# Turned tiles kept interleaved: wide runs through DRAM, and products that read every fourth or eighth element

## The chip, the cores and the metric

The kernel runs on one core of a Trainium2 chip. The metric is the device time of one execution in microseconds, taken as the median of three runs. The times below that are called profiled come from one further execution, recorded by the hardware profiler.

The core has a matrix engine (TensorE, PE in the profile), whose weight loads are shown apart (PEld), a vector engine (VectorE, DVE), a scalar engine (ScalarE, ACT), a general one (GpSimd, POOL) and a queue that issues the transfers (SyncE, SP). A matmul has a stationary operand, which a weight load brings into the array, and a moving operand, which streams through it.

## The reference

64 graphs share one 256x256 adjacency matrix `adj`; each has 256 nodes with 128 features, all in float32. Four layers follow one another, each as `x = layernorm(x + layer(x))`:

```python
# layer 0, five steps (a gated recurrent unit on the graph)
m_in = einsum('nm,bmd->bnd', adj, h)          # m_out is the same, both matrices are adj
u3 = h @ u3_w.T + u3_b
z = sigmoid(av @ w3_w.T + w3_b + u3)          # av = concat(m_in, m_out)
r = sigmoid(av @ w4_w.T + w4_b + u3)
hv = tanh(av @ w5_w.T + w5_b + (r * h @ u5_w.T + u5_b))
h = (1 - z) * h + z * hv
# layer 1: softmaxed mask A; diagonal with W[0], the rest with W[1], and a bias
# layer 2: attention over the edges, times adj, then a two-layer network with norms
# layer 3: sum over k = 0..3 of adj^k x V_k (two equal Chebyshev stacks)
```

## The kernel before

The 64 graphs are taken as 32 pairs. One pair's activations are a tile of 128 partitions and 512 floats: four pieces of 128x128 (two graphs, two halves of the nodes each). The tile exists in two layouts. In the token layout, partitions are nodes; in the feature layout, partitions are features. A matmul contracts over the partitions, so a product with a weight matrix wants the feature layout and a product with `adj` wants the token layout, and the kernel turns tiles from one to the other all the time.

**How a tile is turned (`turn`, L557).** For the last pairs TensorE does it against an identity (L566). For all others it goes by DMA, in four steps: VectorE transposes the tile in blocks of 32x32 (L572, `STREAM_TRANSPOSE`); SP sends the result to a DRAM tile `d` of class E (L574), written so that each of the four pieces lies in one block of 128x128; then four transfers (L580, one per group of 32 partitions) fetch it back with blocks and partitions exchanged. Each run of consecutive bytes fetched is 32 floats, 128 bytes. What comes back is the turned tile with its four pieces one after another along the partition. One tile per pair, the attention weights `u`, is twice as wide (1024 floats, eight pieces) and is turned in the same way, back into itself.

**Where turned tiles are read.** `h` in layer 0, steps 2 to 5 (by `spread7`, L596, or by `spread`, L585, for the first pair; after the fifth step only by the addition at L755); `dT` in layer 1 (`products`, L758); `xT` in layer 2 (L824), the attention weights `wT` (L864) and `zT` (`products`); `xT` in layer 3 (`polynomial7`, L947, or L906 for the last two pairs). In all of these products the piece of the turned tile is the stationary operand, so it goes through a weight load.

**`spread7`** multiplies by a 256x256 matrix held as 2x2 blocks with seven products instead of eight. Three sums are formed first on VectorE or GpSimd (L615 to L617). Of the seven products (L609), three take a piece of the tile itself as stationary operand: `H(0, 0)`, `H(0, 1)` and `H(1, 1)`; four take a sum.

**Order of the work.** The program is not written in the order in which it runs. Each operation is handed to a planner (`Schedule`, L115) with an assumed duration for each engine that could do it. `order` (L163) picks, again and again, the ready operation that could start first and, among equals, the one that is due first, and fixes from this one order for every engine's queue. The list `SEEDS` (L63) perturbs the due times in each window of 15 us. For a transfer, the assumed times are a triple of wait, moving time and time after. Each queue on the chip then runs in that fixed order and waits on semaphores.

Of the kernel before, what the change touches and what calls it, by code (L numbers as in the profile page):

```python
# [12 lines left out]
P = 128  # L13
# [12 lines left out]
L1 = -1  # L26
# [36 lines left out]
SEEDS = [0, 113, 389, 2033, 10562, 18537, 0, 26210, 32078, 38683, 45160, 51706, 59435, 64921, 73141, 0, 83634, 0,  # L63
         0, 101285, 106383, 115324, 122347, 124837, 135500, 136596, 144091, 154692, 155685, 163406, 167552, 0,
         184910, 185838, 194559, 198013, 204219, 214550, 217961, 222675, 234550, 236036, 241268, 247877, 256254,
         259921, 269567, 275378, 0, 285335, 290367, 299853, 303332, 311190, 314874, 321452, 333089, 337426,
         340720, 349168, 0, 0, 0, 0, 0, 0, 0, 0, 0, 0, 0, 0, 426668, 0, 438032, 447771, 0, 460174, 0, 468597,
         475031, 0, 0, 497766, 503314, 0, 0, 520395, 524746, 0, 0, 545845, 549434, 555392, 562168, 571415, 574768,
         578884, 0, 0]
# [7 lines left out]
class Value:  # L77
# [3 lines left out]
    def __init__(self, cls=None, ap=None, name="v"):  # L81
        self.cls, self.ap, self.name = cls, ap, name
        self.writers, self.readers, self.left = [], [], 0


        self.seeded = self.full = False
# [153 lines left out]
def kernel(ctx: ExitStack, tc: tile.TileContext, x, xT, adj, adjT, mats, cols, rows, out):  # L240
# [305 lines left out]
    def tokens(v):  # L546
        return v.at(4, D)

    def to_sbuf(t, name):
        v = Value("A", name=name)  # L550
        evacuate(lambda: v.at(512), lambda: t.at(512), [t], [v])
        return v
# [4 lines left out]
    def turn(i, name, site, n=512):  # L557


        o = Value("A", name=name) if n == 512 else i  # L560
        if not by_dma(site):
            ts = [Value("PS", name="ps") for _ in range(n // 512)]
            for k, t in enumerate(ts):
                def fn(k=k, t=t):
                    for c in range(4):
                        nc.tensor.transpose(tokens(t)[:, c, :], i.at(n // P, P)[:, 4 * k + c, :], ident.ap)  # L566
                pe(TURN, fn, [i, ident], [t])
            for k, t in enumerate(ts):
                evacuate(lambda k=k: o.at(n)[:, 512 * k:512 * k + 512], lambda t=t: t.at(512), [t], [o])
            return o  # L570
        st, d = Value("A" if n == 512 else "B", name="turn"), Value("E", name="turn")
        dve(n / 512 * 0.55 + 0.09, lambda: nc.vector.transpose(st.at(n), i.at(n)), [i], [st])  # L572
        blocks = lambda *ap: bass.AP(tensor=d.ap.tensor, offset=d.ap.offset, ap=ap)
        S.add([("SP", 0.52, lambda: nc.sync.dma_start(blocks([P, P], [P * P, n // P], [1, P]), st.at(n // P, P)))],  # L574
              [st], [d], (0.6, n / 512 * 0.86, 0.5))

        def move():
            for q in range(4):
                b = blocks([P, 32], [32 * P, n // 32], [1, 32])
                nc.sync.dma_start(o.at(n // 32, 32)[32 * q:32 * q + 32],  # L580
                                  bass.AP(tensor=b.tensor, offset=b.offset + 32 * q, ap=b.ap))
        S.add([("SP", 2.1 if n == 512 else 2.7, move)], [d], [o], (-0.8, n / 512 * 1.5, 0.9))
        return o

    def spread(i, right):  # L585

        t = bank()
        for b in range(2):
            def fn(b=b):
                for j in range(2):  # L590
                    nc.tensor.matmul(t.at(2, N)[:, b, :], tokens(i)[:, 2 * b + j, :], right.ap[:, j, :],  # L591
                                     start=(b == j == 0), stop=(j == 1), skip_group_check=True)
            pe(mm(256, 2), fn, [i, right, *[t] * b], [t])
        return t

    def spread7(h, right, terms):  # L596
# [6 lines left out]
        H = lambda b, j: lambda: blk(h, 2 * b + j)  # L603
# [11 lines left out]
        sum_(0.335, 0.69, lambda e: e.tensor_sub(sv.at(4, P)[:, 0:2], h.at(4, P)[:, 0::2], h.at(4, P)[:, 2:4]), [h], [p1])  # L615
# [104 lines left out]
    def layer0(x0, hT):  # L720
# [34 lines left out]
        dve2(TT, lambda: nc.vector.tensor_add(y.at(512), h.at(512), x0.at(512)), [h, x0], [y])  # L755
        layer_norm(y, x0)

    def products(lefts, rights, t=None):  # L758

        first, t = t is None, t or bank()  # L760
        for c in range(4):
            def fn(c=c):
                for k, (i, w) in enumerate(zip(lefts, rights)):
                    nc.tensor.matmul(tokens(t)[:, c, :], tokens(i)[:, c, :], w(), start=(first and k == c == 0),  # L764
                                     stop=(k == len(lefts) - 1), skip_group_check=True)
            pe(mm(128, len(lefts)), fn, [*lefts, W1, *[t] * bool(c or not first)], [t])
        return t

    def layer1b(x1):
        xT = turn(x1, "xT", "x1")  # L770
        xb, rr = Value("A", name="xb"), Value("A", name="rr")
        dve_or_pool(lambda e: e.tensor_add(tokens(xb), tokens(x1), row("l1_bias", 4)), [x1, rbc], [xb])
        ts = []
        for i in range(2):
            t = bank()

            def fn(i=i, t=t):
                for b in range(2):
                    nc.tensor.matmul(t.at(2, 2, D)[:, :, b, :], tokens(xT)[:, 2 * b + i, :], W1.ap[:, i_w:i_w + 2, :], start=(b == 0),
                                     stop=(b == 1), skip_group_check=True)  # L780
            pe(mm(256, 2), fn, [xT, W1], [t])
            evacuate(lambda i=i: rr.at(2, N)[:, i], lambda t=t: t.at(512)[:, N:], [t], [rr], (0.28, 0.34))
            part = lambda t=t: t.at(2, 2, D)[:, 0]
            dve(0.335, lambda i=i, part=part: nc.vector.scalar_tensor_tensor(
                part(), part(), dcol.ap[:, i:i + 1], xb.at(2, 2, D)[:, :, i, :], op0=ALU.mult, op1=ALU.add), [t, dcol, xb], [t])
            ts.append(t)
        for i, t in enumerate(ts):
            def fn(i=i, t=t):
                for j in range(2):
                    nc.tensor.matmul(t.at(512)[:, :N], offT.ap[:, j, i * P:(i + 1) * P], rr.at(2, N)[:, j],  # L790
                                     start=False, stop=(j == 1), skip_group_check=True)
            pe(mm(256, 2), fn, [offT, rr, t], [t])
        s, rs = scale_stats([(t, range(i, 4, 2)) for i, t in enumerate(ts)])
        for i, t in enumerate(ts):
            scale_tokens(t, x1, range(i, 4, 2), s, rs)

    def layer1(x1):
        if S.pair >= n_pairs - L1:
            return layer1b(x1)
# [15 lines left out]
    def layer2(x2):  # L815
# [3 lines left out]
        for b in range(2):  # L819
            t = Value("PS", name="ps")  # L820

            def fn(b=b, t=t):
                for i in range(2):
                    nc.tensor.matmul(t.at(2, D + 2)[:, i, :], tokens(xT)[:, 2 * b + i, :], wpx.ap, start=True, stop=True)  # L824
            pe(mm(130, 2), fn, [xT, wpx], [t])
            dve(0.35, lambda b=b, t=t: nc.vector.tensor_add(hs()[:, 2 * b:2 * b + 2, :], t.at(2, D + 2),
                                                            hbias.ap[:, None, :].to_broadcast([P, 2, D + 2])), [t, hbias], [h])
# [32 lines left out]
        for b in range(2):  # L860
            def fn(b=b, t=t):
                for it in range(2):
                    for jt in range(2):
                        nc.tensor.matmul(tokens(t)[:, 2 * b + it, :], wT.at(8, P)[:, 4 * b + 2 * it + jt, :],  # L864
# [26 lines left out]
    def layer3(x3, p):  # L891
# [7 lines left out]
        for i in range(2):  # L899
            t = bank()  # L900

            def fn(i=i, t=t):
                for b in range(2):
                    c = 2 * b + i
                    pr = t.at(2, 2, D)[:, :, b, :]
                    nc.tensor.matmul(pr, tokens(xT)[:, c, :], vx.ap, start=(b == 0), stop=False, skip_group_check=True)  # L906
# [40 lines left out]
    def polynomial7(xT, qT, p):  # L947
# [5 lines left out]
        x0, x1, q0, q1 = (lambda: half(xT, 0)), (lambda: half(xT, 1)), (lambda: half(qT, 0)), (lambda: half(qT, 1))  # L953
# [4 lines left out]
        sum_(0.335, 0.69, lambda e: e.tensor_sub(S3(), x0(), x1()), [xT], [s3])  # L958
        sum_(0.335, 0.69, lambda e: e.tensor_sub(S2(), q1(), S3()), [qT, s3], [s2])
        sum_(0.335, 0.69, lambda e: e.tensor_add(S1(), x1(), q1()), [xT, qT], [s1])  # L960
# [4 lines left out]
        def product(v, k, left, right, r, start=False):  # L965
            def fn():
                for i in range(2):
                    nc.tensor.matmul(tokens(v)[:, 2 * k + i, :], left()[:, i * P:(i + 1) * P], right(), start=start and i == 0,  # L968
                                     stop=True, skip_group_check=True)
            pe(mm(128, 2), fn, [*r, vx, vq, vt, *[v] * (not start)], [v])  # L970

        VX, VQ, VT = (lambda k, v=v: (lambda: v.ap[:, k, :]) for v in (vx, vq, vt))
        R = lambda b: rr.at(2, 2, D)[:, :, b, :]
        blocks = lambda v, k: v.at(2, 2, D)[:, k]
        product(y, 0, x0, VX(0), [xT, s2], start=True)
        product(y, 1, S2, VT(1), [s2])
        product(t, 0, S1, VT(0), [s1], start=True)
# [3 lines left out]
        product(y, 1, S3, VT(2), [s3])  # L981
        product(y, 0, q0, VQ(0), [qT])
        evacuate(lambda: half(sv, 0), lambda: half(y, 1), [y], [sv], (0.28, 0.335))
        product(y, 1, q1, VT(3), [qT])
        dve(0.335, lambda: nc.vector.tensor_add(R(1), blocks(t, 0), blocks(sv, 0)), [t, sv], [rr])
        product(t, 0, S4, VQ(1), [s4])
# [103 lines left out]
```

## Time and profile before

| | |
|---|---|
| median of three runs | 1476.21 us (1476.14 to 1479.29) |
| the profiled execution | 1476.42 us |
| its span, first to last instruction | 1474.2 us |
| granted TensorE clock | 0.999 |
| TensorE busy | 1462.0 us in 8274 passes |
| weight loads | 8274, 1068.6 us busy, beside the matmuls |
| VectorE, ScalarE, GpSimd busy | 1293.2, 1078.7, 1010.0 us |
| DMA, queue of SP | 946704 packets, 214.81 MB, 71.3% of 16 engines |

One execution is profiled and its span, plus 2.2 us around it, is its time. Each float32 product of the program appears as two passes, each a weight load and a matmul, so the 512 products of L764 are 1024 in the profile. A row of groups gives the source line, the engine, the operation, the written and the read tiles by name (without buffer numbers), the shapes, the count, and after the bar the busy time in us and the mean duration of one in ns. Passes overlap, so count times mean is more than the busy time; the spacing of starts is what one pass costs.

### The profile page before, as it was taken

How to read it: one execution, taken by the hardware profiler on the slowest of the kernel's cores; microseconds unless marked ns; L12 is line 12 of the kernel's file. 1: busy time of each engine (PE TensorE's matmuls, PEld its weight loads, DVE VectorE, ACT ScalarE, POOL GpSimd, SP SyncE). 2: the span in 40 equal slices, each digit the busy share in tenths (PEclk: the TensorE clock that was granted, in tenths of full speed). 3: DMA queues.
4: the chain of work that ended last, by engine and by line, in shares of the span. 5: the costliest groups of instructions: out<-in, count | busy, mean ns of one | idle time of the engine just before them, and what ended most of it. 6: DMA issues, size and time to landing. Idle time of an engine off the chain costs nothing.

```text
span 1474.2 us, 29700 instructions
## 1 busy us (share of the span) xinstructions
PE 1462.0 (99%) x8274; PEld 1068.6 (72%) x8274; DVE 1293.2 (88%) x3185; ACT 1078.7 (73%) x3315; POOL 1010.0 (69%) x1574
## 2 busy tenths in 40 slices
PE   9999999999999999999999999999999999999998
PEld 6565666667667777777668777667777677778997
DVE  7877878889999989999988988888999889899995
ACT  3444556667788788878766887666788777889896
POOL 4422445566677788877658787657778788779875
PEclk9999999999999999999999999999999999999999
DMA  7544565767788898778786677675897777766653
GB/s 227 115 103 87 119 130 117 155 133 157 152 166 168 180 187 161 164 152 165 160 157 140 143 171 159 124 152 124 170 177 158 156 146 149 160 138 135 127 106 93
DMA packets 946868, 216.70 MB, mean 147 GB/s; under 512 B 726032, under 2 KB 942224, under 8 KB 946704
## 3 DMA queue, kind: packets, MB, share of 16 engines
q1 hardware_dynamic: 946704, 214.81, 71.3%
q8 instruction: 66, 1.08, 0.3%
q14 instruction: 98, 0.80, 0.2%
HBM read 116.86 MB, written 97.85 MB: 146 GB/s over the span
## 4 chain that ended last, share of the span: by engine, by line
PE 93%; DVE 3%; POOL 2%; ACT 1%; DMA 1%; issue 1%; SPq 0%; POOLq 0%; ACTq 0%; DVEq 0%
PE ps L609 24%; PE ps L735 9%; PE ps L742 9%; PE ps L743 9%; PE ps L727 9%; PE ps L728 9%; PE ps L764 7%; PE ps L968 6%; PE ps L864 3%; PE ps L1011 3%; PE ps L591 2%; PE ps L824 2%; POOL s L696 1%; DVE b L839 0%; POOL s L651 0%
## 5 line engine op out<-in xcount | busy, mean ns | idle before, releaser
L609 PEld LDWEIGHTS ps<-aT,a 128*128 128x128 f32 x2208 | 297.3, 192 | 78.2 <-issue 69.1
L273 ACT COPY a<-ps 128x128 f32<-128x128 f32 (+2 forms) x618 | 259.5, 442 | 105.2 <-PE ps L609 49.2
L609 PE MATMUL ps<-aT,a 128*128 128x128 f32 x2208 | 324.3, 275 | 0.5 <-ACT x L708 0.5
L731 ACT ACTIVATE a<-ps,bzrh 128x512 f32<-128x512 f32 x160 | 110.5, 691 | 102.4 <-PE ps L728 92.8
L746 ACT ACTIVATE ps<-ps,bzrh 128x512 f32<-128x512 f32 x160 | 106.2, 664 | 98.0 <-PE ps L743 95.6
L628 POOL TENSOR_TENSOR a<-a 128x128 f32<-128x128 f32 x206 | 105.2, 516 | 90.8 <-DVE a L624 80.1
L742 PE MATMUL ps<-a,w 128*128 128x512 f32 x320 | 163.8, 594 | 0.0
L728 PE MATMUL ps<-a,w 128*128 128x512 f32 x320 | 163.4, 592 | 0.0
L743 PE MATMUL ps<-a,u5h 128*128 128x512 f32 x320 | 163.4, 592 | 0.0
L735 PE MATMUL ps<-a,w 128*128 128x512 f32 x320 | 162.8, 594 | 0.1
L630 DVE TENSOR_TENSOR a<-ps,a 128x256 f32<-128x256 f32 x239 | 99.1, 417 | 71.0 <-ACT a L273 42.1
L688 ACT ACTIVATE a<-ps 128x128 f32<-128x128 f32 x504 | 133.1, 289 | 29.7 <-PE ps L764 13.4
L572 DVE STREAM_TRANSPOSE a<-a 128x512 f32<-128x512 f32 x215 | 149.4, 699 | 3.7 <-POOL a L1028 0.5
L696 POOL TENSOR_TENSOR s<-s,neg_half 128x4 f32<-128x4 f32 x127 | 142.4, 1122 | 6.8
L764 PE MATMUL ps<-W,a 128*128 128x128 f32 x1024 | 142.1, 275 | 0.1
L624 POOL TENSOR_TENSOR a<-a 128x256 f32<-128x256 f32 x123 | 92.0, 750 | 72.9 <-ACT a L273 72.1
L764 PEld LDWEIGHTS ps<-W,a 128*128 128x128 f32 x1024 | 130.3, 192 | 14.5 <-issue 12.4
L737 ACT ACTIVATE a<-ps,bzrh 128x512 f32<-128x512 f32 x160 | 110.8, 692 | 37.4 <-PE ps L735 34.3
L727 PE MATMUL ps<-a,W 128*128 128x512 f32 x256 | 131.0, 593 | 0.9 <-ACT a L273 0.9
L615 POOL TENSOR_TENSOR a<-a 128x256 f32<-128x256 f32 x97 | 72.3, 746 | 64.8 <-DMA a<-e 44.2
L743 PEld LDWEIGHTS ps<-a,u5h 128*128 128x128 f32 x320 | 60.8, 190 | 76.5 <-issue 64.8
L728 PEld LDWEIGHTS ps<-a,w 128*128 128x128 f32 x320 | 60.8, 190 | 76.5 <-issue 65.3
(255 smaller groups left out, 3650.7 us busy)
## 6 DMA issues: line engine op xcount, KB each, us to landing
e<-a SPq DMA_DIRECT2D x277, 256.0 KB
a<-e SPq DMA_DIRECT2D x1108, 64.0 KB
e<-b SPq DMA_DIRECT2D x32, 512.0 KB
b<-e SPq DMA_DIRECT2D x128, 128.0 KB
x<-x_in SPq DMA_DIRECT2D x32, 256.0 KB
t<-xT_in SPq DMA_DIRECT2D x32, 256.0 KB
a<-d SPq DMA_DIRECT2D x32, 256.0 KB
y_out<-a SPq DMA_DIRECT2D x31, 256.0 KB
```

Source lines behind the costliest of these rows:

```text
L273: S.add([("ACT", us[0], lambda: nc.scalar.copy(o(), i())), ("DVE", us[1], lambda: nc.vector.tensor_copy(o(), i()))], r, w)
L572: dve(n / 512 * 0.55 + 0.09, lambda: nc.vector.transpose(st.at(n), i.at(n)), [i], [st])
L609: pe(mm(128), lambda: nc.tensor.matmul(blk(t, k), left(), rt(), start=start, stop=True, skip_group_check=True), [*r, right, terms, *[t] * ...
L688: nc.scalar.activation(tokens(junk)[:, c, :], v.at(len(tiles), D)[:, k, :], AF.Square, scale=D ** -0.5, accum_out=mv()[:, c, 1:2])
L696: pool(1.02, lambda: nc.gpsimd.tensor_tensor(rs(), rs(), neg_half.ap, op=ALU.pow), [s, neg_half], [s])
L727: nc.tensor.matmul(t.at(512), mat("u3"), hT.at(512), start=True, stop=False)
L728: nc.tensor.matmul(t.at(512), w4.ap, mT.at(512), start=False, stop=True)
L735: pe(mm(512), lambda t=t, mT=mT: nc.tensor.matmul(t.at(512), w3.ap, mT.at(512), start=False, stop=True, skip_group_check=True), [w3, mT, t ...
L737: act(0.59, lambda t=t, z=z: nc.scalar.activation(z.at(512), t.at(512), AF.Tanh, bias=bzrh.ap[:, 0:1], scale=0.5), [t, bzrh], [z])
L742: nc.tensor.matmul(t.at(512), w5.ap, mT.at(512), start=True, stop=False)
L743: nc.tensor.matmul(t.at(512), u5h.ap, r.at(512), start=False, stop=True)
L764: nc.tensor.matmul(tokens(t)[:, c, :], tokens(i)[:, c, :], w(), start=(first and k == c == 0), stop=(k == len(lefts) - 1), skip_group_chec ...
```

## The change

Turned tiles are no longer stored as pieces one after another. After the change, element `f` of piece `c` lies at position `4 f + c` of the partition (`8 f + c` in the wide tile).

- VectorE's block transpose now takes the 32x32 blocks in the same order but writes its result with a step of four (eight) elements.
- The transfer to DRAM writes each partition as one run of 512 (1024) floats; each of the four transfers back reads runs of `n / 4`, so 128 (256) floats.
- The planner's assumed moving times for these two become 0.76 and 0.8 per 512 columns, from 0.86 and 1.5.
- A value that was turned by DMA is marked `turned`. Two helpers, `chunk` and `chunks`, give one piece or several in either layout, and every reader of a turned tile uses them. Sums over pieces (`spread7`, `polynomial7`, L755) read the turned tile with the step and write contiguously.
- `SEEDS` is a new list, and the unused variant `layer1b` (with the constant `L1`) is gone.

```diff
-SEEDS = [0, 113, 389, 2033, 10562, ...
+SEEDS = [0, 101, 386, 1734, 0, ...
-        self.seeded = self.full = False
+        self.seeded = self.full = self.turned = False
+    def chunk(v, c, n=4):
+        return v.at(P, n)[:, :, c] if v.turned else v.at(n, P)[:, c, :]
+    def chunks(v, *c):
+        return v.at(P, 4)[:, :, slice(*c)].rearrange("p f c -> p c f") if v.turned else v.at(4, P)[:, slice(*c)]
 def turn(i, name, site, n=512):
...
-        dve(n / 512 * 0.55 + 0.09, lambda: nc.vector.transpose(st.at(n), i.at(n)), [i], [st])
-        blocks = lambda *ap: bass.AP(tensor=d.ap.tensor, offset=d.ap.offset, ap=ap)
-        S.add([("SP", 0.52, lambda: nc.sync.dma_start(blocks([P, P], [P * P, n // P], [1, P]), st.at(n // P, P)))],
-              [st], [d], (0.6, n / 512 * 0.86, 0.5))
+        k, w = n // P, n // 4
+        dve(n / 512 * 0.55 + 0.09, lambda: nc.vector.transpose(st.at(4, 32, k).rearrange("p q e c -> p c q e"), i.at(k, 4, 32)), [i], [st])
+        line = lambda start, *ap: bass.AP(tensor=d.ap.tensor, offset=d.ap.offset + start, ap=ap)
+        S.add([("SP", 0.52, lambda: nc.sync.dma_start(line(0, [n, P], [1, n]), st.at(n)))], [st], [d], (0.6, n / 512 * 0.76, 0.5))
         def move():
             for q in range(4):
-                b = blocks([P, 32], [32 * P, n // 32], [1, 32])
-                nc.sync.dma_start(o.at(n // 32, 32)[32 * q:32 * q + 32],
-                                  bass.AP(tensor=b.tensor, offset=b.offset + 32 * q, ap=b.ap))
-        S.add([("SP", 2.1 if n == 512 else 2.7, move)], [d], [o], (-0.8, n / 512 * 1.5, 0.9))
+                nc.sync.dma_start(o.at(4, w)[32 * q:32 * q + 32], line(q * w, [n, 32], [32 * n, 4], [1, w]))
+        S.add([("SP", 2.1 if n == 512 else 2.7, move)], [d], [o], (-0.8, n / 512 * 0.8, 0.9))
+        o.turned = True
...
-        H = lambda b, j: lambda: blk(h, 2 * b + j)                       # spread7
+        H = lambda b, j: lambda: chunk(h, 2 * b + j)
-        sum_(..., lambda e: e.tensor_sub(sv.at(4, P)[:, 0:2], h.at(4, P)[:, 0::2], h.at(4, P)[:, 2:4]), [h], [p1])
+        sum_(..., lambda e: e.tensor_sub(sv.at(4, P)[:, 0:2], chunks(h, 0, 4, 2), chunks(h, 2, 4)), [h], [p1])
-        dve2(TT, lambda: nc.vector.tensor_add(y.at(512), h.at(512), x0.at(512)), [h, x0], [y])
+        dve2(TT, lambda: nc.vector.tensor_add(tokens(y), chunks(h, 0, 4), tokens(x0)), [h, x0], [y])
-                    nc.tensor.matmul(tokens(t)[:, c, :], tokens(i)[:, c, :], w(), ...     # products; likewise L591, L824, L906
+                    nc.tensor.matmul(tokens(t)[:, c, :], chunk(i, c), w(), ...
-                        nc.tensor.matmul(..., wT.at(8, P)[:, 4 * b + 2 * it + jt, :],
+                        nc.tensor.matmul(..., chunk(wT, 4 * b + 2 * it + jt, 8),
-        product(y, 0, x0, VX(0), [xT, s2], start=True)                    # polynomial7
+        product(y, 0, lambda i: chunk(xT, i), VX(0), [xT, s2], start=True)
```

## The prediction

> **What bounds the kernel now.** I read the page's busy times first, then the groups of TensorE by shape, then its timeline at two places, then the idle time by stage.
>
> ```profile
> PE 1462.0 (99%) x8274; PEld 1068.6 (72%) x8274; DVE 1293.2 (88%) x3185; ACT 1078.7 (73%) x3315; POOL 1010.0 (69%) x1574
> ...
> L609 PEld LDWEIGHTS ps<-aT,a 128*128 128x128 f32 x2208 | 297.3, 192 | 78.2 <-issue 69.1
> ...
> L609 PE MATMUL ps<-aT,a 128*128 128x128 f32 x2208 | 324.3, 275 | 0.5 <-ACT x L708 0.5
> ```
>
> TensorE is busy for 1462 of 1474 us, and 0.5 us of idle time stand before the 2208 passes of its largest group. Matmul ends are modelled, so I checked with the starts: over 1466.7 us from first to last pass, starts are 112 ns apart after a 128-wide pass (6446 passes), 216 after a 256-wide, 430 after a 512-wide. Those spacings fill 1462.6 us; what exceeds them is 8.8 us. So nothing is to be had from shorter waits beyond some 9 us, and anything that lengthens a pass is paid in full.
>
> What sets the 112 ns? First the timeline of weight loads and matmuls (start, length, engine, line), in the thick of it:
>
> ```profile
> 699.82 0.75 PEld L609 LDWEIGHTS ps<-aT,a 128*128 128x128 f32 x6
> ...
> 699.93 0.83 PE L609 MATMUL ps<-aT,a 128*128 128x128 f32 x6
> ```
>
> Six loads of 192 ns take 0.75 us: (750 - 192) / 5 = 112 ns apart; the matmuls likewise, (830 - 275) / 5 = 111. Load k+1 runs while pass k streams. Now a place where TensorE had been idle:
>
> ```profile
> 494.08 1.12 PE L727 MATMUL ps<-a,W 128*128 128x512 f32 x2 [0.90 <-ACT a L273]
> 495.05 1.02 PE L728 MATMUL ps<-a,w 128*128 128x512 f32 x2
> ...
> 495.05 0.19 PEld L728 LDWEIGHTS ps<-a,w 128*128 128x128 f32 x1 [0.24 <-issue]
> ```
>
> The two passes of L727 begin 0.97 us before the next pair, not 0.86: the first load lay bare. In the records the first spacing is 534 ns where 430 is usual. A contiguous load of 128 columns thus costs **104 ns** when nothing covers it, and a 128-wide pass covers 112. The slack is 8 ns. The last row shows that under 512-wide passes a load sits idle 0.24 us: it is fetched one pass ahead and no further, so slack of wide passes isn't saved up.
>
> Where TensorE is idle (stretch: length, PE busy, PEld, DVE, ACT, POOL, clock, DMA share, GB/s):
>
> ```profile
> 600.00:800.00 200.00, 200.00 (x1149) 145.83 (x1149) 180.75 (x433) 150.45 (x461) 145.63 (x231) 1.00 0.77 157
> ...
> 1400.00:1474.20 74.20, 68.13 (x511) 64.41 (x509) 55.63 (x170) 59.56 (x243) 47.46 (x77) 0.98 0.48 101
> ```
>
> None in the middle; half of the 12 us in the last stage.
>
> [...] the trace has 13.4 ns per 128 B packet against 29.5 per 512 B. No trace of before has a load, or a VectorE write, with such a step.
>
> **The change part by part.**
>
> *Stepped weight loads.* The program has 1064 products whose stationary operand was turned by DMA: layer 0 360 (three of seven, 30 pairs, four steps) and 16 for the first pair, dT 128, xT 120, wT 256, zT 116, layer 3 60 and 8. Of these 24 are 256 wide: 216 ns cover a doubled load. The other 1040 (784 at step four, 256 at eight) are two passes each, 2080. In the built order 106 of the first passes follow a 256- or 512-wide pass and are covered, which leaves 1974. Price per load: [...] 208 ns, **104 more**: 1974 x 0.104 = **+205 us**, all on TensorE's path. [...]
>
> *Stepped transposes.* 277 of 512 columns (699 ns) and 32 of 1024 (1228). [...] *Stepped sums and additions:* about 68 halves at L615 on VectorE, 32 of 512 columns at L755, some 60 small ones, [...] At nothing under a TensorE of 1474 + 205, which hides it; without that cover it is rival two. GpSimd's L615 (84 on tiles `a`, 746 ns) and its small sums grow too[...].
>
> *Transfers.* As many issues on SP (309 out, 1236 back, near 0.45 us each), no queue passed, no wait added. About 698,000 packets of 128 B become 142,000 of 512 B and 16,000 of 1 KB; the way out goes from 512 B to 2 and 4 KB. With the packets' times (13.4, 29.5, 55, 129 ns and some 220 for 4 KB) that is about 4.0 ms less over 16 engines, the share 71% down to 54%. Tiles land earlier; worth at most the 9 us above, of which the transfers are a part (in a chain over 480 to 540 us, their share is 8.5%). I take -2 to nothing, since the transpose ahead is as much later.
>
> *New order.* The same 4171 products and 1715 transfers; VectorE gets 40 instructions fewer, GpSimd 18 and ScalarE 11 more. About -8 and +13 us beside 181 and 464 idle: nothing. `layer1b` was never called.
>
> Sum: span 1474.2 + 205 = 1679, plus 2.2 around it: **1681 us**. The profiled execution (1476.4) is 0.2 above the median of the runs.
>
> **Rivals.**
>
> *One: a step of 16 bytes is free* on TensorE's load and on VectorE's write [...]. It decides if the stepped load stays under 112 ns, 8 above now. For it: half a microsecond more on transposes could vanish in 181 us of idle VectorE, and the transfers are truly lighter. [...] Then only the waits move: half of the 5 us lost between 200 and 1400 us and some of the last 6: **1471**, own range 1466 to 1480. This is the one on the other side.
>
> *Two: TensorE is free, VectorE is not.* [...] in an order made for 0.70 us transposes: about **1540**. [...]
>
> *Three: only the step of eight costs* [...]: 510 passes x 0.104 = 53, **1529**.
>
> **How the numbers follow.** 0.50 for the forecast (own range 1600 to 1765), 0.33 for rival one, 0.10 and 0.07 for the others. Below 1467 lies a tenth of rival one, above 1765 a sixth of the forecast case: the range is 1467 to 1765. Rival one splits into 0.19 faster, 0.08 same, 0.06 slower, by 0.2% (3 us, about what a measurement of this kernel can tell from no change); the rest is slower, 0.73.
>
> **What would show it.** Right: L609's loads with mean well over 192 ns and those of wT (L864) and dT most, starts near 216 ns apart behind them; loads in L728 or L743 unchanged; PE still at 99%; [...] DMA near 54%. Wrong: loads at 192 ns throughout; then read the transposes: at 0.70 it is rival one, above 1 us with TensorE idle on VectorE it is two. What I could have wrong most is the size: [...]

## The result, and the profile after

| | before | after |
|---|---|---|
| median of four runs | 1477.59 us (1476.14 to 1479.29) | **1715.79 us** (1713.68 to 1716.82) |
| ratio | | 1.161 (1.159 to 1.163) |
| profiled execution, its span | 1476.42, 1474.2 us | 1715.96, 1713.9 us |

The changed kernel is 16% slower, 238 us. The prediction was 1681 us in a range of 1467 to 1765, with 0.73 for slower; its likeliest case has happened, and its size is short by 35 us.

The page of the kernel after, busy times and groups (a row: line, engine, operation, tiles, shapes, count, then busy us and mean ns, then idle time ahead of it). All lines from `turn` on stand some lines lower or higher than before: L609 is now L615, L572 is L580, L864 is L840, L743 is L749.

```profile
PE 1701.8 (99%) x8274; PEld 1322.4 (77%) x8274; DVE 1428.7 (83%) x3145; ACT 1094.5 (64%) x3330; POOL 1026.2 (60%) x1592
...
L615 PEld LDWEIGHTS ps<-aT,a 128*128 128x128 f32 x2208 | 384.8, 235 | 73.0 <-issue 48.8
L615 PE MATMUL ps<-aT,a 128*128 128x128 f32 x2208 | 399.5, 310 | 3.5 <-POOL a L621 2.4
...
L580 DVE STREAM_TRANSPOSE a<-a 128x512 f32<-128x512 f32 x215 | 238.9, 1119 | 2.0 <-ACT a L714 0.2
...
L840 PE MATMUL ps<-h,b 128*128 128x128 f32 x512 | 131.0, 401 | 0.0
...
L840 PEld LDWEIGHTS ps<-h,b 128*128 128x128 f32 x512 | 126.6, 333 | 0.9 <-DVE s L651 0.2
L749 PEld LDWEIGHTS ps<-a,u5h 128*128 128x128 f32 x320 | 60.6, 190 | 77.3 <-issue 64.6
```

The same groups of loads and transposes in the kernel before:

```profile
L864 PEld LDWEIGHTS ps<-h,b 128*128 128x128 f32 x512 | 61.8, 192 | 1.1 <-DVE a L572 0.5 <-issue 0.5
L743 PEld LDWEIGHTS ps<-a,u5h 128*128 128x128 f32 x320 | 60.8, 190 | 76.5 <-issue 64.8 <-DVE a L630 1.2 <-DVE ps L748 1.0
...
L572 DVE STREAM_TRANSPOSE a<-a 128x512 f32<-128x512 f32 x215 | 149.4, 699 | 3.7 <-POOL a L1028 0.5 <-ACT a L708 0.4 <-PE ps L609 0.3
```

TensorE has the same 8274 passes and the same 99%, but is busy for 1701.8 us: it doesn't wait more, its passes take longer. The loads of L840, all stepped by eight, take 333 ns where they took 192, while those of L749, which no edit touched, stay at 190. The 235 of L615 is a mean over loads of two kinds, adjacent ones of 192 ns and stepped ones of 308 to 332. The block transposes went from 699 to 1119 ns.

The same eight products of the attention weights, one after another: weight loads in the timeline of the kernel before,

```profile
749.67 0.97 PEld L864 LDWEIGHTS ps<-h,b 128*128 128x128 f32 x8
```

and loads and matmuls in that of the kernel after:

```profile
906.04 1.99 PEld L840 LDWEIGHTS ps<-h,b 128*128 128x128 f32 x8
...
906.15 2.07 PE L840 MATMUL ps<-h,b 128*128 128x128 f32 x8
```

Before, (970 - 192) / 7 = 111 ns from load to load; after, (1990 - 333) / 7 = 237. The matmuls follow at the loads' pace, (2070 - 401) / 7 = 238: the array waits for weights.

Over the whole trace, 1986 passes of 128 or 130 columns start 180 to 280 ns before the next one, 233.7 on average; before there were 20. Their surplus over 112 ns is 241.7 us (before: 2.0). That is 239.7 more, and the span grew by 239.7.

### The profile page after: what moved, and what is told of

Its sections match the earlier page's. It is cut to its first block, busy times and chain, and to the rows that moved or that the text cites. A ratio compares the mean times of both kernels' runs of the same rounds, so it can differ in the third digit from the quotient of the medians.

```text
span 1713.9 us, 29595 instructions
## 1 busy us (share of the span) xinstructions
PE 1701.8 (99%) x8274; PEld 1322.4 (77%) x8274; DVE 1428.7 (83%) x3145; ACT 1094.5 (64%) x3330; POOL 1026.2 (60%) x1592
## 3 DMA queue, kind: packets, MB, share of 16 engines
q1 hardware_dynamic: 271504, 214.81, 40.9%
## 4 chain that ended last, share of the span: by engine, by line
PE 95%; DVE 2%; POOL 1%; issue 1%; DMA 0%; ACT 0%; SPq 0%; POOLq 0%; DVEq 0%; ACTq 0%
PE ps L615 25%; PE ps L770 10%; PE ps L748 8%; PE ps L749 8%; PE ps L741 8%; PE ps L733 8%; PE ps L734 8%; PE ps L840 7%; PE ps L945 6%; PE ps L800 3%; PE ps L989 2%; PE ps L597 1%; DMA W<-mats_in 0%; POOL a L621 0%; DVE a L580 0%
## 5 line engine op out<-in xcount | busy, mean ns | idle before, releaser
L615 PEld LDWEIGHTS ps<-aT,a 128*128 128x128 f32 x2208 | 384.8, 235 | 73.0 <-issue 48.8
L615 PE MATMUL ps<-aT,a 128*128 128x128 f32 x2208 | 399.5, 310 | 3.5 <-POOL a L621 2.4
L272 ACT COPY a<-ps 128x512 f32<-128x512 f32 (+2 forms) x625 | 261.7, 437 | 218.8 <-PE ps L615 126.0
L580 DVE STREAM_TRANSPOSE a<-a 128x512 f32<-128x512 f32 x215 | 238.9, 1119 | 2.0 <-ACT a L714 0.2
L770 PEld LDWEIGHTS ps<-W,a 128*128 128x128 f32 x1024 | 190.2, 255 | 15.1 <-issue 13.2
L770 PE MATMUL ps<-W,a 128*128 128x128 f32 x1024 | 201.1, 332 | 0.0
L630 POOL TENSOR_TENSOR a<-a 128x256 f32<-128x256 f32 x146 | 111.2, 765 | 108.2 <-ACT a L272 107.5
L749 PE MATMUL ps<-a,u5h 128*128 128x512 f32 x320 | 163.6, 593 | 0.1
L743 ACT ACTIVATE a<-ps,bzrh 128x512 f32<-128x512 f32 x160 | 110.5, 691 | 52.5 <-PE ps L741 47.6
L702 POOL TENSOR_TENSOR s<-s,neg_half 128x4 f32<-128x4 f32 x127 | 136.5, 1075 | 6.7
L840 PE MATMUL ps<-h,b 128*128 128x128 f32 x512 | 131.0, 401 | 0.0
L840 PEld LDWEIGHTS ps<-h,b 128*128 128x128 f32 x512 | 126.6, 333 | 0.9 <-DVE s L651 0.2
L749 PEld LDWEIGHTS ps<-a,u5h 128*128 128x128 f32 x320 | 60.6, 190 | 77.3 <-issue 64.6
```

The source lines that it names most:

```text
L272: S.add([("ACT", us[0], lambda: nc.scalar.copy(o(), i())), ("DVE", us[1], lambda: nc.vector.tensor_copy(o(), i()))], r, w)
L615: pe(mm(128), lambda: nc.tensor.matmul(blk(t, k), left(), rt(), start=start, stop=True, skip_group_check=True), [*r, right, terms, *[t] * ...
L702: pool(1.02, lambda: nc.gpsimd.tensor_tensor(rs(), rs(), neg_half.ap, op=ALU.pow), [s, neg_half], [s])
L749: nc.tensor.matmul(t.at(512), u5h.ap, r.at(512), start=False, stop=True)
L770: nc.tensor.matmul(tokens(t)[:, c, :], chunk(i, c), w(), start=(first and k == c == 0), stop=(k == len(lefts) - 1), skip_group_check=True)
L840: nc.tensor.matmul(tokens(t)[:, 2 * b + it, :], chunk(wT, 4 * b + 2 * it + jt, 8), hs()[:, 2 * b + jt, :D], start=(b == it == jt == 0), st ...
```

## The experiments

Eight kernels were run. In their diffs only the core of an edit is shown. Where one run stands for a kernel, it is the profiled one. Ratios are to runs of the kernel before that were taken beside each experiment (medians of 1476.4 to 1476.9 us).

**1. Only the loads put back.** In the changed kernel, products read adjacent elements.

```diff
-        product(0, H(0, 0), B(0, 0), [h], start=True)
+        product(0, L(0, 0), B(0, 0), [h], start=True)   # L: load_of(h, 2 * b + j); likewise at every product
+    def load_of(v, c, n=4):
+        return v.at(n, P)[:, c, :]
```

> The changed kernel, but every product reads the turned tile's pieces as 128 adjacent elements, as before the change (the products get wrong numbers; transposes, sums, transfers and order stay as changed). Theory (the stepped weight loads make the time, 121 ns more for each pass that nothing covers): all loads at 192 ns, passes 112 ns apart, and nearly all of the 238 us is gone: 1475 to 1510 us. What is left above 1476 is the price of VectorE's stepped writes without their cover: VectorE is then busy some 1429 of some 1490 us. Rival (the slower transposes or the new order hold TensorE up, the long loads only lie beside it): 1600 us or more.

Measured: 1518.18 us, 1.0278 (1.0258 to 1.0297) of before. 198 of the 238 us are gone, and the rest is more than was expected, by 8 us. From its page and its groups of TensorE:

```profile
PE 1478.7 (98%) x8274; PEld 1071.7 (71%) x8274; DVE 1415.7 (93%) x3145; ACT 1082.0 (71%) x3330; POOL 1046.9 (69%) x1592
...
L620 PE MATMUL ps<-aT,a 128*128 128x128 f32 x2208 | 325.4, 276 | 7.3 <-POOL a L626 3.0 <-DVE a L626 2.3 <-DVE a L628 0.7
L753 PE MATMUL ps<-a,w 128*128 128x512 f32 x320 | 164.2, 595 | 5.7 <-DVE a L761 2.6 <-DVE a L641 2.3 <-DVE a L864 0.6
```

The matmuls are back at 276 ns. VectorE is at 93% and TensorE now waits for it and for GpSimd (L626 is the first sum, L761 the end of a recurrent step). This is the second rival of the prediction, laid bare. Over the whole run VectorE is busy for 1416 of 1515 us, but that is an average. In two stretches (columns as in the prediction; the kernel before first, then this one)

```profile
400.00:600.00 200.00, 197.86 (x1149) 145.33 (x1148) 186.01 (x470) 163.82 (x522) 158.69 (x238) 1.00 0.86 171
```

```profile
400.00:600.00 200.00, 191.77 (x1099) 139.31 (x1098) 197.60 (x435) 156.31 (x497) 158.96 (x235) 1.00 0.53 162
...
1200.00:1400.00 200.00, 193.34 (x1215) 151.31 (x1214) 196.08 (x474) 159.48 (x551) 158.17 (x227) 1.00 0.45 136
```

VectorE is busy for 98 to 99% of the time, and TensorE loses 6.7 to 8.2 us in each. There VectorE's own time is the bound, or close to it. The order of work, which was planned with transposes of 0.64 us, may cost some of the rest; the two were not separated.

**2. Only the step put into the kernel before.**

```diff
-        product(0, H(0, 0), B(0, 0), [h], start=True)
+        product(0, L(0, 0), B(0, 0), [h], start=True)   # L: load_of(h, 2 * b + j); likewise at every product that reads a turned tile
+    def load_of(v, c, n=4):
+        return v.at(P, n)[:, :, c] if v.turned else v.at(n, P)[:, c, :]
...
+        o.turned = True
```

> The kernel before, with one thing of the change: products read the turned tile with a step of four, or eight for the attention weights (the tile isn't interleaved, so the numbers are wrong). Theory: some 1985 passes at 234 ns instead of 112, the rest as before: 1476 + 1985 x 0.122 = 1718 us, and VectorE's transposes stay at 0.70 us. Rival (the step costs only together with the slower transposes or the new order): below 1600.

Measured: 1709.71 us, once. 1979 passes have the long spacing, 233.8 ns on average, and VectorE's busy time is what it was:

```profile
PE 1699.8 (100%) x8274; PEld 1322.7 (77%) x8274; DVE 1297.1 (76%) x3185; ACT 1089.0 (64%) x3315; POOL 998.3 (58%) x1574
```

The step in the weight loads makes some 233 us of the 238 by itself, with old transposes, old transfers and old order.

**3. Only the transposes put back.**

```diff
-        dve(..., lambda: nc.vector.transpose(st.at(4, 32, k).rearrange("p q e c -> p c q e"), i.at(k, 4, 32)), [i], [st])
+        dve(..., lambda: nc.vector.transpose(st.at(n), i.at(n)), [i], [st])
```

> The changed kernel, but VectorE's block transposes write adjacent elements (the pieces come back wrongly arranged, so the numbers are wrong); stepped loads and sums stay. Theory (VectorE's slower transposes cost nothing as long as the stepped loads cover them, though 40 us without that cover): 1706 to 1716 us, as the changed kernel. Rival (the two costs add): 1716 - 40 = 1676.

Measured: 1709.83 us, once, with transposes of 699 ns and VectorE busy for 1317.5 us. So under the stepped loads the slower transposes cost some 6 us; it is one run, and the four of the changed kernel spread over 3 us. The costs don't add: with the loads put back as well (experiment 4) the time is 1474, against 1518 with the loads alone, so that without cover VectorE's steps, sums and addition included, cost 44.

**4. Only the transfers and the order.** Adjacent elements throughout:

```diff
-        dve(..., lambda: nc.vector.transpose(st.at(4, 32, k).rearrange("p q e c -> p c q e"), i.at(k, 4, 32)), [i], [st])
+        dve(..., lambda: nc.vector.transpose(st.at(n), i.at(n)), [i], [st])
-        o.turned = True
```

> The changed kernel without any step: transposes write, and sums and products read, adjacent elements; what stays is the wide runs through DRAM, the planner's new transfer times and the new order (the pieces are wrongly arranged, so the numbers are wrong). Theory: lighter transfers are worth at most the 9 us that TensorE's starts lose before: 1468 to 1478 us, DMA share near 46%, transposes at 0.70 us. Rival (the transfers are worth nothing, or the new order is worse): 1478 to 1490.

Measured: 1474.30 us over 22 runs, 0.9981 (0.9974 to 0.9988). That is 2.6 us, within the ceiling of some 9 us of late starts. To see which of its two parts gained them, both were crossed. First the kernel before with the new order:

```diff
-SEEDS = [0, 113, 389, ...        ...  (0.6, n / 512 * 0.86, 0.5)   ...  (-0.8, n / 512 * 1.5, 0.9)
+SEEDS = [0, 101, 386, ...        ...  (0.6, n / 512 * 0.76, 0.5)   ...  (-0.8, n / 512 * 0.8, 0.9)
```

> The kernel before with the planner's inputs of the changed one (the list of seeds and the two transfer times), so with its order of work on every engine, but with the old transfers in runs of 128 bytes and no step anywhere; the result is the reference's. It splits the 2.6 us that wide runs and new order gained together. If the wide runs gained them: 1477 us or more, since this order counts on transfers that aren't there. If the new order gained them: 1474.

Measured: 1492.03 us, 1.0104 (1.0089 to 1.0119). Then the reverse, wide runs in the old order (experiment 4 with the old seeds and times):

> Wide runs through DRAM as in the run with transfers only, no step anywhere, but with the planner's inputs, and so the order, of the kernel before (the pieces are wrongly arranged, so the numbers are wrong). It closes the square of two orders and two kinds of transfer. An order made for slow transfers has nothing to wait for when they are faster: 1472 to 1477 us. If the lighter transfers were worth the same 18 us here as in the new order, it would fall to 1465, which is below the 1462.6 us of spaced starts plus head and tail, so that can't be.

Measured: 1472.79 us, 0.9975 (0.9965 to 0.9985).

| | runs of 128 bytes | wide runs |
|---|---|---|
| old order | 1476.4 | 1472.8 |
| new order | 1492.0 | 1474.3 |

The lighter transfers gain in both orders, 4 us in the old one and 18 in the new one, which counts on them. The waits of the first sum for a fetched tile go the same way. From the lists of waits (engine, line, what it waited for: us in total, times, longest), with runs of 128 bytes in the old order and then in the new one:

```profile
POOL a L615 <- DMA a<-e: 44.2, 22, 7.1
DVE a L615 <- DMA a<-e: 4.9, 3, 2.3
```

```profile
POOL a L615 <- DMA a<-e: 54.3, 28, 6.6
DVE a L615 <- DMA a<-e: 19.1, 26, 1.6
```

With wide runs, in the old order and then in the new one, where VectorE's wait is no longer among the 60 longest:

```profile
POOL a L620 <- DMA a<-e: 29.7, 13, 6.5
```

```profile
POOL a L620 <- DMA a<-e: 27.4, 9, 6.3
```

The new order itself is 16 us slower than the old one with runs of 128 bytes, and with wide runs not told from it (0.9981 and 0.9975 of before, with intervals that overlap). In this scheme of turning a tile, the wide runs can't be had with adjacent pieces: it is the interleaving that makes the runs wide.

**5. Other steps.** One run to measure loads at steps of two and three and of adjacent elements with a shifted start, and transposes at a step of two.

```diff
+    def load_of(v, c, n=4, way="threes"):
...
+        if way == "twos":                                   # xT of layer 2, attention weights
+            return v.at(n // 2, P, 2)[:, c // 2, :, c % 2]
+        return v.at(512)[:, c:c + 3 * P - 2:3] if way == "threes" else v.at(512)[:, 1 + 127 * c:129 + 127 * c]
...
+        # 512-wide transposes: from i.at(2, 2, P) to st.at(2, P, 2).rearrange("p g f e -> p g e f")
```

> A measurement of other steps, on the changed kernel; products read the wrong elements. Layer 0's pieces are read with a step of three elements, layer 2's xT and the attention weights with a step of two, the pieces in the common product routine as 128 adjacent elements that start one element off; the 512-wide transposes write with a step of two, the wide ones still with eight. [...] loads of 192 ns at step two, about 325 or somewhat less at step three, 192 with the odd start, transposes of 0.70 us at step two. [...]

The formula of the shifted start, `1 + 127 * c`, takes the four pieces from elements 1, 128, 255 and 382, so that they start at all four places of a group of four elements.

Measured (the run took 1534.56 us, once), from its groups of loads (L849 step two, L779 shifted start, L954 still step four) and transposes (L588, 512 wide at step two, 1024 wide at step eight):

```profile
L849 PEld LDWEIGHTS ps<-h,b 128*128 128x128 f32 x512 | 65.1, 197 | 1.1 <-issue 0.7 <-DVE s L658 0.2 <-ACT a L272 0.2
...
L779 PEld LDWEIGHTS ps<-W,a 128*128 128x128 f32 x1024 | 131.2, 192 | 15.8 <-issue 14.6 <-ACT b L836 0.2 <-ACT a L723 0.2
...
L954 PEld LDWEIGHTS ps<-vx,a 128*128 128x128 f32 x120 | 30.4, 324 | 0.8 <-DVE h L811 0.4 <-issue 0.2
```

```profile
L588 DVE STREAM_TRANSPOSE a<-a 128x512 f32<-128x512 f32 x215 | 150.2, 702 | 2.1 <-PE ps L757 0.2 <-ACT a L723 0.2
L588 DVE STREAM_TRANSPOSE b<-b 128x1024 f32<-128x1024 f32 x32 | 65.7, 2053 | 0.0
```

The usual time (median) from the start of a narrow pass to the start of the next, by the step of its own load, where the pass before it is narrow too; a step of eight is from the kernel after, a step of four the same in both:

| step (elements) | 1 | 2 | 3 | 4 | 8 |
|---|---|---|---|---|---|
| ns from pass to pass | 112 | 118 | 175 | 233 | 238 |
| ns per element of the step | 112 | 59 | 58 | 58 | 30 |

A step of two costs 6 ns, a step of three 63, a step of four 121, and eight 5 more than four. From a step of two to a step of four, the time goes with the step: 118 / 2, 175 / 3 and 233 / 4 are 59, 58 and 58 ns. Adjacent elements, at 112, and a step of eight, at 238, don't follow it. The proportion is measured; its cause was not shown, nor why it ends at four.

**6. The whole kernel at a step of two**, as a test of the 6 ns that a step of two costs.

```diff
-        return v.at(P, n)[:, :, c] if v.turned else v.at(n, P)[:, c, :]
+        return v.at(n // 2, P, 2)[:, c // 2, :, c % 2] if v.turned else v.at(n, P)[:, c, :]   # likewise the transposes and sums
```

> The changed kernel with a step of two in place of four or eight in every transpose, sum and product (pieces interleaved two and two; the transfers are as changed, so the pieces come back wrongly arranged and the numbers are wrong). [...] each narrow pass behind such a load 118 ns, 6 more than with adjacent elements, so 1474.3 + 1974 x 0.006 = 1486 us (1482 to 1492), transposes 0.70 us also for the wide ones at 1.23. If instead the cost grew evenly with the step, a step of two would cost a third of a step of four: some 1550.

Measured: 1485.89 us, 1.0063 (1.0046 to 1.0079), wide transposes of 1.23 us. The 6 ns per pass account for the 11.6 us over the 1474.3 of adjacent elements: 1969 narrow passes behind a narrow one are followed after 118.1 ns on average. The sums that read with this step took what they take with adjacent elements (the first one 418 ns on VectorE, 419 before). Even so little is a loss here, since TensorE has no time to give. A kernel with the right result in this layout was not run: its pieces would come back in runs of 256 bytes, and there is no reason to expect it below this time.

## Why the prediction was right, and where it was short

*What bounds the kernel:* right. A longer load is paid pass by pass, and 239.7 us more of long spacings made the span longer by 239.7.

*The slack of 8 ns:* wrong, though it changed little. It set a bare load of 104 ns, after idle time, against 112 ns taken as the time of a pass. But the kernel before has passes of one column, with loads of 128 columns as everywhere, behind a 512-wide pass:

```profile
229.37 0.28 PE L475 MATMUL ps<-asd,rep 128*128 128x1 f32 x2
229.51 0.36 PE L476 MATMUL ps<-ccol,W 128*128 128x1 f32 x2
229.73 0.36 PE L477 MATMUL ps<-ccol,W 128*128 128x1 f32 x2
229.95 1.10 PE L742 MATMUL ps<-a,w 128*128 128x512 f32 x2
```

The wide pass covered the load of the first of the six, and the next starts 28 ns later; the others start 112 ns apart, like passes of 128 columns. And a narrow pass whose load a 512-wide pass has covered is followed after 109 ns (314 such passes). So the 112 ns are the pace of the loads, one after another, and not of the passes: the loads set the pace of narrow passes already before the change, and nothing was left to hide a longer one.

*A sum on the way:* 6462 narrow passes at 112 ns, 211 at 216 and 1600 at 430 fill 1457.3 of the 1466.7 us, not 1462.6. The 9 us that exceed them stand. With 1.2 us ahead of the first start, 6.3 behind the last and 2.2 around the span, the floor that the expectation for wide runs in the old order speaks of is 1467, and its 1465 still lies below.

*The count:* exact. In the kernel after, 2080 narrow passes have a load of over 300 ns; 106 of them stand behind a wide pass and are followed after 109 to 126 ns, so their load was covered, and 1974 are not. (The 1986 long spacings have a few others among them, as before.) Not covered, against the prediction, were the loads of 256-wide passes: those passes start 233 ns apart in place of 216. They are so few that it makes under 1 us.

*The price of a load* is the term that was mis-sized: 104 ns more were taken, 121.7 are measured. The step that failed is the doubling of the bare load of 104 to 208 ns: it was the author's assumption, and no trace of before showed it. Loads one after another take 112; half their rate would be 224, and 233 are measured. There was also luck in it: in the prediction's own terms, a load of 208 ns under a pass of 112 adds 96, not 104, and the sum would have been 1666. With 1974 x 0.122 it would have been 1474.2 + 241 + 2.2 = 1717.

*VectorE:* 1428.7 us measured, against 1293.2 before. The steps made 144.7 us of it (1284.0 without any, in experiment 4); what they would cost was not shown by any trace of before. The new order took 9 us off, which the prediction had as "about -8". The transposes take 0.82 ns more per column (420 ns over 512). L755's addition grew by 0.80 ns per column (714 to 1123 ns), and the first sum on VectorE usually takes 614 ns where it took 419, 0.76 per column; its mean grew less, since tiles that weren't turned by DMA are among them. GpSimd's sums were to grow. Its first one got shorter with two stepped sources, usually 661 ns in place of 727, and the small ones grew by some 65. "Hides it at nothing" was right to 6 us.

*Transfers:* worth at most 9 us and in sum nothing, which held for this kernel: 2.6 us with the order that goes with them. The DMA share fell to 40.9%, not 54%, for two reasons: the span is longer (at an equal span, in experiment 4, the share is 47.3%), and the wide packets were dear in the estimate (2 KB took 93 ns, not 129; 4 KB 167, not 220).

*Rivals.* One, the free step, is out (experiments 2 and 5); its time of 1471 is nearly that of the two runs with adjacent elements and wide runs, 1472.8 and 1474.3, which are what it would have been. Two, VectorE alone, is real as a mechanism, 1518 us against 1540, the author's estimate, but covered. Three, only the step of eight, is out: four and eight cost the same within 5 ns.

## What to carry to other kernels

Before a layout is made cheaper for the transfers, ask at what rate each engine reads it. On a kernel that TensorE bounds, look at passes whose load is known to be covered and compare them with the rest: here 109 ns against 112 says that the loads set the pace of narrow passes, so that a longer load is paid in full (239.7 us more of long spacings made the span 239.7 longer). For float32, a step of two elements was nearly free here for weight loads (6 ns per pass), and free for VectorE's transposes (702 ns against 699) and sums (418 against 419); a step of four was free for neither (121 ns per pass, 420 per transpose), nor a step of three for loads (63 ns per pass). A gain on a resource that isn't the bound, 24 points of DMA share at an equal span, was worth 2.6 us here, with the order that goes with it (experiment 4). And an order planned for faster transfers lost 16 us without them and gained nothing with them.

## What had not been expected of the hardware

A weight load with a step of two float32 elements is almost as fast as an adjacent one (197 ns against 192, passes 118 ns apart against 112), and adjacent elements are loaded equally fast from whichever of four elements they start (192). Passes of one column, each with its own load of 128 columns, are no faster than passes of 128 columns (112 ns apart), unless their load has been covered (28 ns). VectorE's block transpose writes with a step of two as fast as adjacent elements (702 ns for 512 columns against 699) and with four and eight at about 0.81 ns more per column, the same for both steps (1119 ns for 512 columns, 2056 for 1024). GpSimd's subtraction of 128x256 takes less time with two sources at a step of 16 bytes than with adjacent ones (usually 661 ns against 727).
